# A graph network with attention on TensorE: one layer's row through DRAM, one normalisation folded into the next, and a new timetable for the attention

## The chip, the cores and the metric

The kernel runs on one core of a Trainium2 chip. The metric is the time of one launch in microseconds on the device. A core has TensorE (PE, matrix products and transposes), VectorE (DVE), ScalarE (ACT), GpSimd (POOL) and SyncE (SP, which here only issues transfers). Each works through its own list of instructions in order and waits on semaphores for the others.

## The reference

There are 64 graphs of 256 nodes with 256 features, and an adjacency matrix of zeros and ones for each. Layer 0 is a gated graph network of three steps; layer 1 is graph attention. Both are added to their input and normalised.

```python
A = (adj != 0)
h = x
for i in range(3):
    m    = h @ weight[i]
    aggr = einsum('bst,bsd->btd', A, m)
    h    = gru(aggr, h)          # r, z sigmoid; n = tanh(i_n + r * h_n); (1 - z) * n + z * h
x = layernorm(x + h)             # eps 1e-5

Wh   = x @ W
e    = leaky_relu((Wh @ a1)[:, :, None] + (Wh @ a2)[:, None, :], 0.2)
attn = softmax(where(adj > 0, e, -9e15), axis=2)
x    = layernorm(x + attn @ Wh)
```

## The kernel before

**Tiling.** Two graphs make a pair, so there are 32 pairs (`NP`) of 512 nodes. The state of a pair is kept transposed in `hT` (features on partitions, 512 nodes along the row). The product with `weight[i]` is folded into the gate weights ahead of time (`fold`, into `wc`), so that a step is an aggregation of `h` and then gate products of 512 columns. Each fp32 operand is cut into a high, a low and a cross part (`upper`, `lower`, `cross`), and a product is a sum over these.

**A block** is one step i of one pair p. `front(p, i)` prepares it: transposes to node order (`turn`), the high part (`split`), the low part (`rest`, `lo`, by POOL for i = 0), the aggregation (`aggregate`, line 340), and the parts of the aggregate and of `hT`. `gates(p, i)` then runs, for each half e of the features, the products r (12 matmuls), n (6), z (12) and t (6), all on line 369. ScalarE copies each out of PSUM (lines 374, 376) and applies sigmoid or tanh (line 387); VectorE adds the cross part (line 378); POOL and VectorE blend (lines 395 to 408).

**The order** is written out by hand. There is a clock in ticks; `at(t, step)` puts a step on a heap, and `tick()`, called after every six gate matmuls, issues all that is due. So the order on each engine is the order in which steps fall due. A block has 12 ticks. The blocks run as (turn, 0), (turn - 1, 1), (turn - 2, 2), which is 36 ticks for a pair; three pairs are under way at a time. While one block's products run, the front of the next is issued between them, by the offsets in the tuples `CLOSE` and `LOOSE`.

**Attention** of a pair starts when its last block's products are issued, and is spread over the 72 ticks that follow:

- `again` reloads the transposed input `vT` from DRAM, where `stash` had put it, and adds `hT` to it.
- `halves`, `back` and `join` turn the sum into node order `v`: both 16-bit halves are set apart, a DMA transpose on SP turns them, and they are joined again.
- `layer_norm` is called on `v`: statistics, a power on POOL (line 423), a shift, and `apply` (line 430).
- `project` (line 493) multiplies `vT` by W and by two further columns, which give s1 and s2; `spread` (lines 502, 504) scales the result by the norm's factor and copies s2, broadcast over 128 columns, into `sc`.
- `rows` (line 512) transposes these copies on TensorE, so that s2 lies along the row in every partition.
- `scores` (line 516), a mask, the row maximum (line 527) and the exponentials (line 530) follow, the last at ticks 47 and 48.
- `weights_T` (line 540) transposes the exponentials at ticks 53 and 54, `combine` (line 548) multiplies them by Wh, and a second `layer_norm` and the store follow.

PSUM has eight banks, used in rotation. Tiles of the attention lie in a pool with one buffer each (`late`; two for `v`). The last two pairs take theirs from buffers that the gates no longer need (`room`). All loads of x and adj, the stash, the reload, the DMA transposes and the store are issued by SP, in order. The weights come on ScalarE's queue and the biases on POOL's.

Of the kernel before, what the change touches and what calls it, by code (L numbers as in the profile page):

```python
# [26 lines left out]
def kernel(  # L27
# [164 lines left out]
    load_x(0)  # L192
    load_adj(0)
    make_identity(nc, ident)
    nc.gpsimd.memset(half, -0.5)
    nc.gpsimd.memset(neg, NEG_INF)
# [11 lines left out]
    def rows_T(src, use):  # L208
        for c in range(C):
            for o0, o1, t in src:  # L210
                pt = bank("pw")
                for o in range(o1 - o0):
                    nc.tensor.transpose(pt[:, o * P:(o + 1) * P], t[:, o, c * P:(c + 1) * P], ident)
                use(c, o0 * P, o1 * P, pt[:, :(o1 - o0) * P])

    def square_T(src, name):
        pt = bank("pw")
        for e in range(C):
            for d in range(C):
                nc.tensor.transpose(pt[:, (e * C + d) * P:(e * C + d + 1) * P],  # L220
                                    src[:, d, e * P:(e + 1) * P], ident)
        dst = work.tile([P, K, P], F32, tag="hi1", name=name, bufs=1)
        nc.scalar.copy(flat(dst), pt)
        return dst.rearrange("p k n -> p (k n)").rearrange("p (e d) -> p e d", e=C)

    def fold(i, wT, d):
        for o0, o1 in ((0, 512), (512, O)):
# [50 lines left out]
    def begin(p):  # L278

        s = pairs[p] = Pair()  # L280
        s.x, s.adj = loaded.pop(p), loaded_adj.pop(p)
        s.A = work.tile([P, G, C, N], F32R, tag="A", name=f"A_{p}", bufs=3)
        nc.vector.tensor_scalar(s.A, s.adj, 0.0, None, op0=ALU.not_equal)
        s.hT = work.tile([P, C, GN], F32, tag="hT", name=f"hT_{p}", bufs=4)
# [6 lines left out]
    def front(p, i, t, pace):  # L291
# [4 lines left out]
        def turn(d):  # L296
            s = pairs[p]
            if i == 0:
                src[d] = nodes(s.x, d)
# [4 lines left out]
        def split(d):  # L304
            hi[d] = work.tile([P, K, P], F32R, tag=f"hi{d}", name=f"hi{d}_{nm}", bufs=1)
            nc.scalar.copy(hi[d], src[d])

        def rest(d):
            lo[d] = work.tile([P, K, P], F32R, tag=f"lo{d}", name=f"lo{d}_{nm}", bufs=1)
            lower(nc.gpsimd if i == 0 else nc.vector, lo[d], src[d], hi[d])  # L310
# [5 lines left out]
        if i == 0:  # L316
            at(t + pace[0][1] + 2, stash)
# [92 lines left out]
    def layer_norm(v, name, t, then=None):  # L410
# [3 lines left out]
        rs = work.tile([P, K], F32, tag="rs_" + name[0], name=f"rs_{name}")  # L414
        nm = work.tile([P, K], F32, tag="nmr_" + name[0], name=f"nmr_{name}")

        def stats(k):
            nc.vector.bn_stats(st[:, k, :], v[:, k // C, k % C, :])
            nc.vector.bn_aggr(mv[:, k, :], st[:, k, :])

        def power():
            nc.gpsimd.tensor_scalar(rs, mv[:, :, 1], EPS, None, op0=ALU.add)
            nc.gpsimd.tensor_tensor(rs, rs, half, ALU.pow)  # L423

        def shift():
            nc.vector.scalar_tensor_tensor(nm, mv[:, :, 0], -1.0, rs, op0=ALU.mult, op1=ALU.mult)

        def apply(k):
            vk = v[:, k // C, k % C, :]
            nc.scalar.activation(vk, vk, AF.Identity, scale=rs[:, k:k + 1], bias=nm[:, k:k + 1])  # L430
# [9 lines left out]
        return rs  # L440

    def attention(p, t):

        s = pairs[p]
        pts = {}

# [3 lines left out]
        at(t + 5, again)  # L450
        at(t + 14, lambda: nc.vector.tensor_add(flat(s.vT), flat(s.vT), flat(s.hT)))

        def halves(d):

# [8 lines left out]
        def back(d):  # L463

            if d == 0:
                s.sc = room("sc", [P, K, N], p)
                s.turned = s.sc.rearrange("p k n -> p (k n)").bitcast(U16).rearrange(
                    "p (h k d) -> p h k d", h=2, k=K)
            nc.sync.dma_start_transpose(
                s.turned.rearrange("p h k d -> p (h k) d")[:, :, d * P:(d + 1) * P],  # L470
                s.apart[:, d].rearrange("p h n -> p (h n)"))

        def join(g):
            if g == 0:
                s.v = room("v", [P, G, C, D], p)
            dst = s.v[:, g].rearrange("p c d -> p (c d)").bitcast(U16).rearrange("p (n h) -> p n h", h=2)
            src = s.turned[:, :, g * C:(g + 1) * C, :].rearrange("p h c d -> p h (c d)")
            nc.scalar.copy(dst[:, :, 0], src[:, 0])
            nc.vector.tensor_copy(dst[:, :, 1], src[:, 1])
        for d in range(C):  # L480
            at(t + 22 + d, lambda d=d: halves(d))
            at(t + 23 + d, lambda d=d: back(d))
        for g in range(G):
            at(t + 29 + g, lambda g=g: join(g))
        at(t + 30, lambda: setattr(s, "rs", layer_norm(s.v, f"a_{p}", (t + 31, t + 33, t + 34, t + 49))))

        def project(k):
            if k == 0:
                s.s1 = work.tile([P, K], F32, tag="s1", name=f"s1_{p}")
                s.s2 = s.sc[:, :, :P]  # L490
# [14 lines left out]
        for k in range(K):  # L505
            at(t + 35 + k, lambda k=k: project(k))
            at(t + 36 + k, lambda k=k: spread(k))

        def rows():
            pts[0] = bank("s2")  # L510
            for k in range(K):
                nc.tensor.transpose(pts[0][:, k * P:(k + 1) * P], s.s2[:, k, :], ident)

        def scores():
            for k in range(K):
                nc.scalar.activation(s.sc[:, k, :], pts[0][:, (k // C) * N:(k // C + 1) * N], AF.Prelu,
                                     bias=s.s1[:, k:k + 1], alpha=ALPHA)
        at(t + 40, rows)
        at(t + 41, scores)

        s.nm = work.tile([P, K], F32, tag="nm", name=f"nm_{p}")
        s.sm = work.tile([P, K], F32, tag="sm", name=f"sm_{p}")
# [3 lines left out]
        at(t + 42, masked)  # L526
        at(t + 43, lambda: nc.vector.tensor_reduce(s.nm, s.sc, AX.X, ALU.max, negate=True))
# [28 lines left out]
        for g in range(G):  # L556
            at(t + 53 + g, lambda g=g: weights_T(g))
            at(t + 54 + g, lambda g=g: nc.vector.tensor_copy(flat(s.sc[:, g * C:(g + 1) * C, :]), pts[g]))
            at(t + 57 + g, lambda g=g: combine(g))
            at(t + 58 + g, lambda g=g: add(g))  # L560
# [4 lines left out]
        at(t + 60, lambda: layer_norm(s.v, f"b_{p}", (t + 61, t + 64, t + 66, t + 70), store))  # L565
# [3 lines left out]
    LOOSE = (2, 3, 4, 6, 7, 8), (5, 8, 10)  # L569
# [5 lines left out]


    rows_T(wh_n, lambda c, o0, o1, pt: cut_weight([t[:, c, o0:o1] for t in whh], pt, f"h{c}_{o0}"))
    begin(0)
    masking(0)
    load_adj(1)  # L580
    rows_T(wi_n, lambda c, o0, o1, pt: evacuate(wih(c, o0, o1), pt))
    nc.vector.tensor_add(b_sum, bi, bh)
    wT = square_T(w_n[0], "wT_0")
    front(0, 0, clock[0], LOOSE)
    for d in range(C):
        fold(0, wT, d)
        tick(3)
# [13 lines left out]
    for n, (p, i) in enumerate(blocks):  # L601
        if n + 1 < len(blocks):
# [43 lines left out]
```

## Time and profile before

| What | Value |
|---|---|
| time, median of 3 runs | 2247.24 us (2246.81 to 2248.58) |
| profiled execution, own time | 2248.91 us |
| its span in the profile | 2247.1 us |
| first gate product starts | 29.5 us |
| last gate product ends | 2181.1 us |
| TensorE busy | 2189.0 us (97%) |
| VectorE, ScalarE, POOL busy | 1728.2, 1556.4, 1535.2 us |

The profile shows one execution. Its own time is 1.8 us longer than its span; the difference lies around the span. "Busy" of TensorE includes time in which pipelined matmuls overlap, so costs of matmuls are read from the start of one to the start of the next. In lists of waits the columns are the total in us, how often, and the longest; in a timeline they are start and duration in us, engine, line, operation, output and input, and in brackets the idle time before with what ended it.

### The profile page before, as it was taken

To read this page: it belongs to the slowest core of one execution; us is meant where nothing else is said; L and a number is where in the kernel's file an instruction comes from. 1 tells how busy PE (TensorE), PEld (TensorE's weight loads), DVE (VectorE), ACT (ScalarE), POOL (GpSimd) and SP (SyncE) were. 2 spreads that over 40 slices of the span, in tenths; PEclk is the share of its full clock that TensorE was granted. 3 is DMA by queue.
4 is the path that set the end of the run, shared out by engine and by line. 5 is a ranking of instruction groups with operands and counts; after the bars stand their busy time and mean duration, and the time that the engine had idled before them with its cause. 6 is when DMAs were issued, how large, how long until landed. Compare 5 with 4: busy or idle time off the path is not lost.

```text
span 2247.1 us, 31126 instructions
## 1 busy us (share of the span) xinstructions
PE 2189.0 (97%) x10724; PEld 1813.6 (81%) x10724; DVE 1728.2 (77%) x2920; ACT 1556.4 (69%) x2899; POOL 1535.2 (68%) x1084
## 2 busy tenths in 40 slices
PE   7999999999999999999999999999999999999985
PEld 5788888888888888888888888888888888888864
DVE  4667778878778878778878778878778878778875
ACT  4566777677777677777677777677777677777665
POOL 5777667767667767667767667767667767667751
PEclk9999999999999999999999999999999999999997
DMA  3011111111111211112111111111111111111111
GB/s 113 29 38 38 34 42 57 57 48 38 42 43 57 57 47 38 41 45 57 57 48 38 41 45 57 57 48 38 40 46 57 57 48 38 39 47 38 29 38 47
DMA packets 130237, 105.30 MB, mean 47 GB/s; under 512 B 70368, under 2 KB 121824, under 8 KB 130080
## 3 DMA queue, kind: packets, MB, share of 16 engines
q1 hardware_dynamic: 128288, 101.47, 15.4%
q8 instruction: 86, 1.41, 0.3%
q10 hardware_dynamic: 1616, 1.57, 0.2%
q14 instruction: 71, 0.58, 0.1%
q0 software_dynamic: 176, 0.27, 0.1%
HBM read 52.96 MB, written 33.55 MB: 39 GB/s over the span
## 4 chain that ended last, share of the span: by engine, by line
PE 85%; POOL 10%; ACT 1%; DVE 1%; DMA 1%; issue 1%; POOLq 0%; SPq 0%; ACTq 0%; DVEq 0%
PE pga L369 42%; PE pgb L369 21%; PE pa L340 7%; PE po L548 5%; PE pwh L493 5%; POOL t L396 3%; PE pt L275 3%; POOL lo L132 2%; POOL t L395 2%; PE pt L540 1%; POOL n L405 1%; POOL n L401 1%; PE pt L269 1%; POOL rs_b L423 1%; DMA adj<-in_adj_dram 1%
## 5 line engine op out<-in xcount | busy, mean ns | idle before, releaser
L395 POOL TENSOR_TENSOR t<-hT,n 128x512 f32<-128x512 f32 x192 | 288.4, 1502 | 540.1 <-ACT n L387 540.0
L369 PE MATMUL pga<-hH,whhH_whh 128*128 128x512 f32 x1152 | 388.8, 418 | 0.0
L369 PE MATMUL pgb<-hD,whhD_whh 128*128 128x512 f32 x1152 | 362.0, 395 | 0.8 <-DVE hD L135 0.8
L369 PE MATMUL pga<-hL,whhL_whh 128*128 128x512 f32 x1152 | 362.3, 395 | 0.0
L405 POOL TENSOR_TENSOR n<-n,t 128x512 f32<-128x512 f32 x192 | 283.8, 1478 | 57.8 <-DVE t L378 45.5
L396 POOL TENSOR_TENSOR t<-t,z 128x512 f32<-128x512 f32 x192 | 280.6, 1461 | 15.1
L374 ACT ACTIVATE r<-pga 128x512 f32<-128x512 f32 x192 | 114.5, 596 | 235.6 <-PE pga L369 193.0
L369 PEld LDWEIGHTS pgb<-hD,whhD_whh 128*128 128x128 f32 x1152 | 216.3, 188 | 53.3 <-DVE hD L135 1.3
L369 PEld LDWEIGHTS pga<-hL,whhL_whh 128*128 128x128 f32 x1152 | 216.3, 188 | 51.6 <-POOL hL L132 0.2
L401 POOL TENSOR_TENSOR n<-n,r 128x512 f32<-128x512 f32 x192 | 252.8, 1317 | 0.8 <-DVE n L378 0.7
L132 POOL TENSOR_TENSOR hL<-hT,hH 128x1024 fp32r<-128x1024 f32 x96 | 243.8, 2540 | 8.9 <-ACT hH L129 8.9
L376 ACT ACTIVATE n<-pga,bh 128x512 f32<-128x512 f32 x192 | 131.6, 685 | 154.3 <-PE pga L369 154.0
L378 DVE SCALAR_TENSOR_TENSOR r<-pgb,r 128x512 f32<-128x512 f32 x192 | 131.7, 686 | 135.1 <-ACT r L374 75.2
L369 PEld LDWEIGHTS pga<-hH,whhH_whh 128*128 128x128 f32 x1152 | 196.0, 189 | 24.1
L340 PE MATMUL pa<-A,lo 128*128 128x256 f32 x768 | 195.9, 287 | 12.5 <-POOL lo L132 12.4
L340 PE MATMUL pa<-A,hi 128*128 128x256 f32 x768 | 196.5, 287 | 0.0
L378 DVE SCALAR_TENSOR_TENSOR n<-pgb,n 128x512 f32<-128x512 f32 x192 | 131.5, 685 | 67.5 <-ACT n L376 64.5
L387 ACT ACTIVATE z<-z,b_sum 128x512 f32<-128x512 f32 x192 | 141.6, 738 | 43.1 <-DVE z L378 42.7
L340 PEld LDWEIGHTS pa<-A,lo 128*128 128x128 f32 x768 | 146.9, 191 | 27.2 <-POOL lo L132 21.6
L378 DVE SCALAR_TENSOR_TENSOR t<-pgb,t 128x512 f32<-128x512 f32 x192 | 131.7, 686 | 38.5 <-ACT t L374 36.4
L135 DVE SCALAR_TENSOR_TENSOR hD<-hH,hT 128x1024 fp32r<-128x1024 f32 x96 | 156.5, 1630 | 0.0
L340 PEld LDWEIGHTS pa<-A,hi 128*128 128x128 f32 x768 | 146.8, 191 | 7.2
(136 smaller groups left out, 5495.6 us busy)
## 6 DMA issues: line engine op xcount, KB each, us to landing
x<-in_x_dram SPq DMA_DIRECT2D x32, 512.0 KB, 3.9
adj<-in_adj_dram SPq DMA_DIRECT2D x32, 512.0 KB, 3.9
xT<-hT SPq DMA_DIRECT2D x32, 512.0 KB, 2.6
vT<-xT SPq DMA_DIRECT2D x32, 512.0 KB, 3.3
out_dram<-v SPq DMA_DIRECT2D x32, 512.0 KB, 2.9
sc<-wh SPq DMA_TRANSPOSE x64, 3.1
w_n<-in_L_gnn_weight_dram ACTq DMA_DIRECT2D x3, 256.0 KB, 10.3
rows_aH<-in_L_gnn_w_ih_dram ACTq DMA_DIRECT2D x1, 512.0 KB, 6.1
```

The source lines that it names most:

```text
L132: eng.tensor_sub(dst, src, hi.bitcast(F32))
L135: nc.vector.scalar_tensor_tensor(dst, hi.bitcast(F32), 1.0 + U, src, op0=ALU.mult, op1=ALU.subtract)
L340: nc.tensor.matmul(pt[:, g * N:(g + 1) * N], h[:, g * C + c, :], s.A[:, g, c, :], start=(n == 0), stop=(n == len(todo) - 1))
L369: nc.tensor.matmul(pt, w[:, d, o * P:(o + 1) * P], m[:, d, :], start=n in (0, ends + 1), stop=n in (ends, len(todo) - 1))
L374: nc.scalar.activation(dst, a, AF.Copy, scale=1.0 + U)
L376: nc.scalar.activation(dst, a, AF.Identity, scale=1.0 + U, bias=bias)
L378: nc.vector.scalar_tensor_tensor(dst, b, -1.0 / U, dst, op0=ALU.mult, op1=ALU.add)
L387: nc.scalar.activation(dst, dst, func, bias=bias)
L395: nc.gpsimd.tensor_sub(t, h, n)
L396: nc.gpsimd.tensor_mul(t, t, z)
L401: after(2, lambda r=r, n=n: nc.gpsimd.tensor_mul(n, n, r))
L405: after(1, lambda n=n, t=t: nc.gpsimd.tensor_add(n, n, t))
```

## The change

1. **s2's row.** For all but the last three pairs, s1 and s2 are kept as small columns (`s12`). The s2 columns (512 elements of 4 bytes) are written to DRAM by SP, and read back broadcast to 128 partitions into `sc` (`rows`, `rows_back`). The transposes on TensorE and the broadcast copies are left out there.
2. **First norm.** `shift` and `apply` are not run on `v`. The attention's divisor is multiplied by the norm's factor instead, and the second norm's eps by its square. The second norm removes the offset.
3. **Timetable.** The ticks of the attention are given by a tuple: `EVEN` over 84 ticks for the first 29 pairs, `BRISK` for pair 29, `FAST` for pairs 30 and 31. In `EVEN` the exponentials stand at ticks 57 and 58 and `weights_T` at 60 and 61.
4. **Last three pairs.** They turn `v` back by transposes on TensorE and make s2's row as before.
5. **Fronts.** The front of a first step splits one tick or two earlier (`FIRST`), `h_cross` comes three ticks earlier, `ones` is apart from `begin`, and mask and adj load come later.
6. **Head.** x is loaded first; the front of pair 0 is interleaved with the weights' transposes; its low parts are by VectorE; an activation at the start loads the table; `fold` runs by parts; `square_T` writes to a buffer of tag "z".

```diff
+    load_x(0)
     wh_n = load_rows(w_hh, ("hH", "hL"), nc.sync)
+    load_adj(0)
     wi_n = load_rows(w_ih, ("aH", "aL"), nc.scalar)
...
-    load_x(0)
-    load_adj(0)
     make_identity(nc, ident)
     nc.gpsimd.memset(half, -0.5)
+    warm = const.tile([P, K], F32, name="warm")
+    nc.scalar.activation(warm, half, AF.Sigmoid)
...
         def rest(d):
-            lower(nc.gpsimd if i == 0 else nc.vector, lo[d], src[d], hi[d])
+            lower(nc.gpsimd if i == 0 and p else nc.vector, lo[d], src[d], hi[d])
...
         def power():
-            nc.gpsimd.tensor_scalar(rs, mv[:, :, 1], EPS, None, op0=ALU.add)
+            if eps is None:
+                nc.gpsimd.tensor_scalar(rs, mv[:, :, 1], EPS, None, op0=ALU.add)
+                nc.gpsimd.tensor_scalar(nm, rs, EPS, None, op0=ALU.mult)
+            else:
+                nc.gpsimd.tensor_add(rs, mv[:, :, 1], eps)
             nc.gpsimd.tensor_tensor(rs, rs, half, ALU.pow)
...
-        at(t[2], shift)
-        for k in range(K):
-            at(t[3] + k // 2, lambda k=k: apply(k))
-        if then:
+        if eps is not None:
+            at(t[2], shift)
+            for k in range(K):
+                at(t[3] + k // 2, lambda k=k: apply(k))
             at(t[3] + 2, then)
...
+        def back_by_pe(d):
+            pts[d] = from_T(s.vT, d)
...
         def rows():
-            pts[0] = bank("s2")
+            s.row = far.tile([K, P], F32, tag="row", name=f"row_{p}", bufs=2)
+            nc.sync.dma_start(s.row.rearrange("k n -> n k"), s.s12[:, 1, :], allow_slow_non_contiguous=True)
+
+        def rows_back():
+            pts["row"] = flat(s.sc[:, C:K, :])
+            nc.sync.dma_start(pts["row"], s.row.rearrange("k n -> (k n)").partition_broadcast(P))
+
+        def rows_by_pe():
+            s.sc = room("sc", [P, K, N], p)
+            pts["row"] = bank("s2")
             for k in range(K):
-                nc.tensor.transpose(pts[0][:, k * P:(k + 1) * P], s.s2[:, k, :], ident)
...
-            at(t + 47 + k // 2, lambda k=k: exps(k))
-        at(t + 52, lambda: nc.vector.reciprocal(s.sm, s.sm))
+            at(T["exp"] + k // 2, lambda k=k: exps(k))
+
+        def divide():
+            nc.vector.tensor_mul(s.sm, s.sm, s.rs)
+            nc.vector.reciprocal(s.sm, s.sm)
+        at(T["turn"], divide)
...
-            at(t + 53 + g, lambda g=g: weights_T(g))
-            at(t + 57 + g, lambda g=g: combine(g))
+            at(T["turn"] + g, lambda g=g: weights_T(g))
+            at(T["combine"] + g, lambda g=g: combine(g))
...
+    # again add halves join stats power project rows scores mask max exp turn combine stats2 power2 shift2 apply2
+    EVEN = 12, 21, 31, 37, 38, 40, 42, 47, 53, 55, 56, 57, 60, 64, 68, 72, 74, 81
+    BRISK = 9, 14, 15, 17, 19, 21, 30, 35, 36, 37, 38, 40, 43, 46, 49, 52, 54, 57
+    FAST = 2, 5, 6, 7, 9, 10, 14, 18, 19, 20, 20, 22, 25, 27, 30, 31, 33, 33
 
     CLOSE = (5, 5, 5, 7, 8, 8), (6, 6, 7)
-    LOOSE = (2, 3, 4, 6, 7, 8), (5, 8, 10)
+    LOOSE = (2, 3, 4, 6, 7, 8), (5, 8, 7)
+    FIRST = (2, 1, 2, 6, 7, 8), (5, 8, 7)
...
     begin(0)
+    front(0, 0, clock[0] + 1, ((0, 1, 2, 9, 11, 12), (7, 8, 13)))
+    tick(2)
+    rows_inp(wi_n[0])
+    tick()
+    rows_hid(wh_n[0])
...
-    front(0, 0, clock[0], LOOSE)
-    for d in range(C):
-        fold(0, wT, d)
-        tick(3)
+    for parts in PARTS:
+        for d in range(C):
+            fold(0, wT, d, (parts,))
+            tick(2)
...
-            front(np_, ni, clock[0], CLOSE if n and np_ == blocks[n - 1][0] else LOOSE)
+                after(4, lambda p=np_: ones(p))
+            front(np_, ni, clock[0], CLOSE if n and np_ == blocks[n - 1][0] else LOOSE if ni else FIRST)
             if ni == 0:
                 after(7, lambda p=np_: load_x(p + 1))
-                after(19, lambda p=np_: masking(p))
-                after(20, lambda p=np_: load_adj(p + 1))
+                hold = 33 if L < np_ else 16
+                after(hold, lambda p=np_: masking(p))
+                after(hold + 1, lambda p=np_: load_adj(p + 1))
...
-            attention(p, clock[0])
+            attention(p, clock[0], EVEN if p < NP - 3 else BRISK if p < NP - 2 else FAST)
```

In the lists of offsets in `FIRST`, `LOOSE` and `CLOSE` the first tuple gives turn, split, rest, aggregate, the aggregate's upper part and its rest; the second gives the upper, lower and cross parts of `hT`.

More of the change, by code (lines that the diff above doesn't have):

```diff
@@ L208, in rows_T @@
     def rows_T(src, use):
+        o0, o1, t = src
         for c in range(C):
[L210 to L214, printed above, removed]
+            pt = bank("pw")
+            for o in range(o1 - o0):
+                nc.tensor.transpose(pt[:, o * P:(o + 1) * P], t[:, o, c * P:(c + 1) * P], ident)
+            use(c, o0 * P, o1 * P, pt[:, :(o1 - o0) * P])
     def square_T(src, name):
@@ L221, in square_T, with fold @@
                                     src[:, d, e * P:(e + 1) * P], ident)
[L222 to L227, printed above, removed]
+        dst = work.tile([P, GN], F32, tag="z", name=name)
+        nc.scalar.copy(dst, pt)
+        return dst.rearrange("p (e d) -> p e d", e=C)
+    PARTS = (0, 512), (512, O)
+    def fold(i, wT, d, parts=PARTS):
+        for o0, o1 in parts:
             pt = bank("pw")
@@ L281, in begin, with ones @@
         s.x, s.adj = loaded.pop(p), loaded_adj.pop(p)
+        s.hT = work.tile([P, C, GN], F32, tag="hT", name=f"hT_{p}", bufs=4)
+    def ones(p):
+        s = pairs[p]
         s.A = work.tile([P, G, C, N], F32R, tag="A", name=f"A_{p}", bufs=3)
         nc.vector.tensor_scalar(s.A, s.adj, 0.0, None, op0=ALU.not_equal)
-        s.hT = work.tile([P, C, GN], F32, tag="hT", name=f"hT_{p}", bufs=4)
     def masking(p):
@@ L298, in turn @@
             if i == 0:
-                src[d] = nodes(s.x, d)
                 to_T(s.x, s.hT, d)
@@ L304, in split @@
         def split(d):
+            if i == 0:
+                src[d] = nodes(pairs[p].x, d)
             hi[d] = work.tile([P, K, P], F32R, tag=f"hi{d}", name=f"hi{d}_{nm}", bufs=1)
@@ L316, in front @@
         if i == 0:
-            at(t + pace[0][1] + 2, stash)
+            at(t + pace[0][0] + 3, stash)
         def h_upper():
@@ L408, in gates, with layer_norm @@
             after(lags[2], lambda n=n, t=t, h=h: nc.vector.tensor_add(h, t, n))
-    def layer_norm(v, name, t, then=None):
+    def layer_norm(v, name, t, eps=None, then=None):
         st = work.tile([P, K, nc.vector.BN_STATS_DIM], F32, tag="st_" + name[0], name=f"st_{name}")
         mv = work.tile([P, K, nc.vector.BN_AGGR_DIM], F32, tag="mv_" + name[0], name=f"mv_{name}")
-        rs = work.tile([P, K], F32, tag="rs_" + name[0], name=f"rs_{name}")
-        nm = work.tile([P, K], F32, tag="nmr_" + name[0], name=f"nmr_{name}")
+        rs = work.tile([P, K], F32, tag="rs_" + name[0], name=f"rs_{name}", bufs=3)
+        nm = work.tile([P, K], F32, tag="nmr_" + name[0], name=f"nmr_{name}", bufs=3)
         def stats(k):
@@ L434, in layer_norm, with attention, copy @@
         at(t[1], power)
-        at(t[2], shift)
-        for k in range(K):
-            at(t[3] + k // 2, lambda k=k: apply(k))
-        if then:
+        if eps is not None:
+            at(t[2], shift)
+            for k in range(K):
+                at(t[3] + k // 2, lambda k=k: apply(k))
             at(t[3] + 2, then)
-        return rs
-    def attention(p, t):
+        return rs, nm
+    def attention(p, t, pace):
         s = pairs[p]
         pts = {}
+        even = pace is EVEN
+        T = {k: t + dt for k, dt in zip(
+            "again add halves join stats power project rows scores mask max exp turn combine "
+            "stats2 power2 shift2 apply2".split(), pace)}
+        def copy(j, dst, src):
+            if even or j % 2:
+                nc.vector.tensor_copy(dst, src)
+            else:
+                nc.scalar.copy(dst, src)
         def again():
@@ L449, in again @@
             nc.sync.dma_start(s.vT, s.far)
-        at(t + 5, again)
-        at(t + 14, lambda: nc.vector.tensor_add(flat(s.vT), flat(s.vT), flat(s.hT)))
+        at(T["again"], again)
+        at(T["add"], lambda: nc.vector.tensor_add(flat(s.vT), flat(s.vT), flat(s.hT)))
         def halves(d):
@@ L466, in back @@
                 s.sc = room("sc", [P, K, N], p)
-                s.turned = s.sc.rearrange("p k n -> p (k n)").bitcast(U16).rearrange(
-                    "p (h k d) -> p h k d", h=2, k=K)
+                s.turned = flat(s.sc).bitcast(U16).rearrange("p (h k d) -> p h k d", h=2, k=K)
             nc.sync.dma_start_transpose(
@@ L475, in join, with norm @@
                 s.v = room("v", [P, G, C, D], p)
[L476 to L479, printed above, removed]
-        for d in range(C):
[L481 to L485, printed above, removed]
+            if even:
+                dst = s.v[:, g].rearrange("p c d -> p (c d)").bitcast(U16).rearrange("p (n h) -> p n h", h=2)
+                src = s.turned[:, :, g * C:(g + 1) * C, :].rearrange("p h c d -> p h (c d)")
+                nc.scalar.copy(dst[:, :, 0], src[:, 0])
+                nc.vector.tensor_copy(dst[:, :, 1], src[:, 1])
+            else:
+                copy(g, nodes(s.v, g), pts[g].rearrange("p (k n) -> p k n", k=K))
+        def back_by_pe(d):
+            pts[d] = from_T(s.vT, d)
+        for d in range(C):
+            if even:
+                at(T["halves"] + d, lambda d=d: halves(d))
+                at(T["halves"] + 1 + d, lambda d=d: back(d))
+            else:
+                at(T["halves"] + d, lambda d=d: back_by_pe(d))
+            at(T["join"] + d, lambda d=d: join(d))
+        def norm():
+            s.rs, s.eps = layer_norm(s.v, f"a_{p}", (T["stats"], T["power"]))
+        at(T["join"] + 1, norm)
         def project(k):
             if k == 0:
-                s.s1 = work.tile([P, K], F32, tag="s1", name=f"s1_{p}")
-                s.s2 = s.sc[:, :, :P]
+                s.s12 = work.tile([P, 2, K], F32, tag="s12", name=f"s12_{p}")
+                if not even:
+                    s.wh = room("wh", [P, G, C, D], p)
+                    s2 = io.tile([P, G, C, D], F32, tag="x", name=f"s2_{p}")
+                    s.s2 = s2[:, 0].rearrange("p c (h n) -> p (c h) n", n=P)
             pts[k] = bank("pwh")
@@ L497, in spread @@
             rs = s.rs[:, k:k + 1]
-            for dst, src in ((s.s1[:, k:k + 1], pts[k][:, D:D + 1]),
-                             (s.s2[:, k, :], pts[k][:, D + 1:D + 2].to_broadcast([P, P])),
-                             (s.wh[:, k // C, k % C, :], pts[k][:, :D])):
+            todo = [(s.s12[:, :, k], pts[k][:, D:D + 2]), (s.wh[:, k // C, k % C, :], pts[k][:, :D])]
+            if not even:
+                todo.insert(1, (s.s2[:, k, :], pts[k][:, D + 1:D + 2].to_broadcast([P, P])))
+            for dst, src in todo:
                 if k < 2:
@@ L505, in attention @@
         for k in range(K):
-            at(t + 35 + k, lambda k=k: project(k))
-            at(t + 36 + k, lambda k=k: spread(k))
+            at(T["project"] + k, lambda k=k: project(k))
+            at(T["project"] + 1 + k, lambda k=k: spread(k))
         def rows():
-            pts[0] = bank("s2")
-            for k in range(K):
[L512 to L522, printed above, removed]
+            s.row = far.tile([K, P], F32, tag="row", name=f"row_{p}", bufs=2)
[3 more added lines that the diff above has]
+            nc.sync.dma_start(pts["row"], s.row.rearrange("k n -> (k n)").partition_broadcast(P))
@@ new lines, in rows_by_pe, with scores @@
+        def rows_by_pe():
+            s.sc = room("sc", [P, K, N], p)
+            pts["row"] = bank("s2")
+            for k in range(K):
+                nc.tensor.transpose(pts["row"][:, k * P:(k + 1) * P], s.s2[:, k, :], ident)
+        if even:
+            at(T["rows"], rows)
+            at(T["rows"] + 1, rows_back)
+        else:
+            at(T["rows"], rows_by_pe)
+        def scores(g):
+            if g == 0:
+                s.nm = work.tile([P, K], F32, tag="nm", name=f"nm_{p}")
+                s.sm = work.tile([P, K], F32, tag="sm", name=f"sm_{p}")
+            for k in range(g * C, g * C + C):
+                nc.scalar.activation(s.sc[:, k, :], pts["row"][:, g * N:(g + 1) * N], AF.Prelu,
+                                     bias=s.s12[:, 0, k:k + 1], alpha=ALPHA)
@@ L524, in masked @@
+        for g in range(G):
+            at(T["scores"] + g * even, lambda g=g: scores(g))
         def masked():
             nc.vector.copy_predicated(flat(s.sc), flat(s.mask), neg.to_broadcast([P, K * N]))
-        at(t + 42, masked)
-        at(t + 43, lambda: nc.vector.tensor_reduce(s.nm, s.sc, AX.X, ALU.max, negate=True))
+        at(T["mask"], masked)
+        at(T["max"], lambda: nc.vector.tensor_reduce(s.nm, s.sc, AX.X, ALU.max, negate=True))
         def exps(k):
@@ L556, in attention @@
         for g in range(G):
-            at(t + 53 + g, lambda g=g: weights_T(g))
-            at(t + 54 + g, lambda g=g: nc.vector.tensor_copy(flat(s.sc[:, g * C:(g + 1) * C, :]), pts[g]))
-            at(t + 57 + g, lambda g=g: combine(g))
-            at(t + 58 + g, lambda g=g: add(g))
+            at(T["turn"] + g, lambda g=g: weights_T(g))
+            at(T["turn"] + 1 + g, lambda g=g: copy(g, flat(s.sc[:, g * C:(g + 1) * C, :]), pts[g]))
+            at(T["combine"] + g, lambda g=g: combine(g))
+            at(T["combine"] + 1 + g, lambda g=g: add(g))
         def store():
@@ L564, in store @@
             del pairs[p]
-        at(t + 60, lambda: layer_norm(s.v, f"b_{p}", (t + 61, t + 64, t + 66, t + 70), store))
+        at(T["combine"] + 3, lambda: layer_norm(
+            s.v, f"b_{p}", [T[k + "2"] for k in ("stats", "power", "shift", "apply")], s.eps, store))
+    EVEN = 12, 21, 31, 37, 38, 40, 42, 47, 53, 55, 56, 57, 60, 64, 68, 72, 74, 81
+    BRISK = 9, 14, 15, 17, 19, 21, 30, 35, 36, 37, 38, 40, 43, 46, 49, 52, 54, 57
+    FAST = 2, 5, 6, 7, 9, 10, 14, 18, 19, 20, 20, 22, 25, 27, 30, 31, 33, 33
     CLOSE = (5, 5, 5, 7, 8, 8), (6, 6, 7)
-    LOOSE = (2, 3, 4, 6, 7, 8), (5, 8, 10)
+    LOOSE = (2, 3, 4, 6, 7, 8), (5, 8, 7)
+    FIRST = (2, 1, 2, 6, 7, 8), (5, 8, 7)
     blocks = []
@@ L574, with rows_hid, rows_inp @@
         blocks += [(turn - i, i) for i in range(L) if 0 <= turn - i < NP]
-    rows_T(wh_n, lambda c, o0, o1, pt: cut_weight([t[:, c, o0:o1] for t in whh], pt, f"h{c}_{o0}"))
+    def rows_hid(part):
+        rows_T(part, lambda c, o0, o1, pt: cut_weight([t[:, c, o0:o1] for t in whh], pt, f"h{c}_{o0}"))
+    def rows_inp(part):
+        rows_T(part, lambda c, o0, o1, pt: evacuate(wih(c, o0, o1), pt))
     begin(0)
+    front(0, 0, clock[0] + 1, ((0, 1, 2, 9, 11, 12), (7, 8, 13)))
[3 more added lines that the diff above has]
+    rows_hid(wh_n[0])
+    tick()
+    rows_inp(wi_n[1])
+    tick()
+    rows_hid(wh_n[1])
+    wT = square_T(w_n[0], "wT_0")
+    nc.vector.tensor_add(b_sum, bi, bh)
+    tick()
+    ones(0)
     masking(0)
     load_adj(1)
-    rows_T(wi_n, lambda c, o0, o1, pt: evacuate(wih(c, o0, o1), pt))
-    nc.vector.tensor_add(b_sum, bi, bh)
-    wT = square_T(w_n[0], "wT_0")
-    front(0, 0, clock[0], LOOSE)
-    for d in range(C):
-        fold(0, wT, d)
-        tick(3)
+    tick()
+    for parts in PARTS:
+        for d in range(C):
+            fold(0, wT, d, (parts,))
+            tick(2)
     tick(10)
```

## The prediction

> **What bounds the kernel now.** First the page's busy table, its slices and the chain that ended last:
>
> ```profile
> PE 2189.0 (97%) x10724; PEld 1813.6 (81%) x10724; DVE 1728.2 (77%) x2920; ACT 1556.4 (69%) x2899; POOL 1535.2 (68%) x1084
> ...
> PEclk9999999999999999999999999999999999999997
> ...
> PE 85%; POOL 10%; ACT 1%; DVE 1%; DMA 1%; issue 1%; POOLq 0%; SPq 0%; ACTq 0%; DVEq 0%
> ```
>
> TensorE is busy 97% at full clock, so between first and last gate (29.5 to 2181.1 us) time changes only through TensorE instructions or TensorE waits. In the chain, the same product starts at 1053.26 and 1120.69: a pair costs 67.44 us. Next the waits of TensorE:
>
> ```profile
> PE pa L340 <- POOL lo L132: 12.4, 28, 4.3
> PE pt L540 <- ACT sc L530: 7.3, 3, 7.0
> PE pw L213 <- DMA rows_hH<-in_L_gnn_w_hh_dram: 6.4, 1, 6.4
> PE s L512 <- ACT sc L502: 5.6, 2, 5.3
> PE po L548 <- DVE sc L558: 4.4, 3, 2.3
> ```
>
> Only the first is in the steady part: one wait per pair, and one of 4.3 in the head. The others are the head (before 29.5) and the tail (after 2181.1). The timeline of TensorE prices a group of transposes and that wait:
>
> ```profile
> 1110.75 0.63 PE L369 MATMUL pga<-aH,wc0H_wc 128*128 128x512 f32 x2
> 1111.21 0.60 PE L512 MATMUL s<-ident,sc 128*128 128x128 f32 x4
> 1111.57 0.71 PE L369 MATMUL pga<-aL,wc0L_wc 128*128 128x512 f32 x2
> ...
> 1092.75 0.28 PE L340 MATMUL pa<-A,hi 128*128 128x256 f32 x1
> 1093.33 0.39 PE L340 MATMUL pa<-A,lo 128*128 128x256 f32 x1 [0.29 <-POOL lo L132]
> 1093.55 0.28 PE L340 MATMUL pa<-A,hi 128*128 128x256 f32 x1
> ```
>
> Read from start to start: a gate matmul is 0.234 us; four transposes take 0.36 and make the next pair of matmuls 0.08 later, 0.44 in all. Around the wait, hi to lo to hi takes 0.80 instead of 0.24: it costs 0.56, not the 0.29 shown as idle.
>
> Last, ScalarE's timeline around the exponentials:
>
> ```profile
> 1122.59 0.60 ACT L374 ACTIVATE z<-pga 128x512 f32<-128x512 f32 x1 [0.42 <-PE pga L369]
> 1123.21 1.28 ACT L530 ACT_TABLE_LOAD   x1
> 1124.50 0.51 ACT L530 ACTIVATE sc<-sc,nm 128x256 f32<-128x256 f32 x1
> ...
> 1126.97 1.08 ACT L430 ACTIVATE v<-v,nmr_a,rs_a 128x256 f32<-128x256 f32 x2
> 1128.07 1.28 ACT L387 ACT_TABLE_LOAD   x1
> ```
>
> Two table loads a pair, one into and one out of the exponentials; two exponentials take 1.1 with their accumulator reads.
>
> **The Trainium skill.** "ScalarE: Activation LUTs", section "What ACT_TABLE_LOAD costs", gives 1283 ns for the load and about 1380 for a drain. The trace agrees on the load (1.28) and not on the drain: 0.02 before it, 0.01 after it. I use 1.29. Its section "Table sets: the hidden batching unit" puts exp and sigmoid in different sets and tanh in both; two loads a pair agree. "DMA: Bandwidth & Descriptors", section "Rules for kernel authors", says that a strided last dimension becomes one descriptor per element, and that a read of what a DMA wrote must wait for it. The new row has 512 elements of 4 bytes; the nearest row here, a_w, also 512, took 7.0 us amid the traffic of the head. The section "Anatomy of one DMA" gives 2.0 fixed, the floor of each of the two transfers.
>
> **The change, part by part.** All against the profiled run: span 2247.1, own time 2248.9; the median of three runs is 2247.2. I apply the differences to the median.
>
> *s2 row.* Of 29 groups of L512 transposes before the last gate, 28 go (order of the two programs: 116 matmuls there before, 4 after): -28 x 0.44 = -12.2. In their place SP issues a write and a broadcast read, and the read waits on SP for the write. Behind it stand vT's reload and the adj load; both are wanted more than nine ticks (some 15 us) later. The copies of s2 that ScalarE (2 x 364 ns) and VectorE (2 x 342) made go; no matmul waited for them in the steady part. The row must land in about 11 us, from the last spread to the scores. Between 2+2 and 7.0+3.3 (the reload of vT took 3.3): it fits, at zero; not below zero, as nothing else is released.
>
> *First norm's apply left out.* -4 x 0.59 us of ScalarE a pair and one shift; one POOL product of 0.23 is added. ScalarE was 69% busy: zero on TensorE, but room.
>
> *FIRST pace.* The split and `lo` of a pair's first step come two ticks earlier for the same aggregate. POOL was late by 0.3 to 0.6; two ticks are 2.8: 27 x 0.56 = -15.1. Next late on POOL is the n,r product, which has no matmul behind it for several ticks. Between -15.1 and 0 if POOL only reorders its queue.
>
> *Exponentials in new ticks.* Before, they stood at ticks 47 and 48 and their transposes at 53 and 54; now 57 and 58, and 60 and 61. ScalarE's order there is now: n from PSUM, load, exponentials 0 and 1, load, sigmoid of r, load, exponentials 2 and 3. So four loads a pair. From the first matmul of that n product as zero: n starts at 1.12 (1139.55 to 1140.67 in the trace) and ends at 1.81; load to 3.10; two exponentials to 4.20; load to 5.50; sigmoid (0.72) to 6.23; load to 7.52; two exponentials to 8.6. TensorE does n (6 matmuls), z (12), t (6): 24 x 0.234 = 5.6, where the first transposes find exponentials 0 and 1 ready; then 0.44 and six matmuls, 1.40: at 7.45 it wants exponentials 2 and 3. It waits 1.0 to 1.1, and the restart costs 0.1 (seen at the lo wait). **A new wait of L540 on ScalarE of about 1.15 a pair**, 29 pairs: +33.4. From below: 0.8 if the next activation overlaps the one before; from above: 1.5 if n starts late. Behind the wait all gates are queued.
>
> *Last three pairs by TensorE.* More transposes before the last gate: four groups, +1.8; three project groups moved ahead of it at 0.87: +2.6. Then the tail of 66.0 us loses the three DMA transposes in a row with their copies. The last pair alone, in steps from rows of this tail (7.3 to its last hT, then 33 of add, transposes, copies, stats, power, spread, scores, mask, max, load and exponentials, combine, norm, store), is 40.5. Laid out with the two pairs before it on the same engines I get 53: -13, between -6 and -20.
>
> *Head.* x is first in the queue; `lo` of pair 0 is on VectorE, no longer behind POOL's weight scalings (4.34 wait); the table is loaded before data come. The wait for hD that set 32.8 ends at about 26: -6.5, between -3 and -9.
>
> *At nothing:* later masking, adj load and `ones`, hidden as before by the adj buffer's period; h_cross three ticks earlier, on VectorE (77%).
>
> Sum: -12.2 - 15.1 + 1.8 + 2.6 + 33.4 = +10.5 between the gates; -6.5 - 13 outside: -9.0. **2238 us.**
>
> **Rivals.**
> 1. *The exponentials are ready in time.* Then the new wait is zero and the rest stays: -22.9 - 6.5 - 13 = -42.4, 2204.8. For it: ScalarE has 31% idle and lost the applies. Against it: the chain above holds only instructions that wait for each other on one engine.
> 2. *The row is late* (ends slower). Write and read in series take over 11 us; the scores then hold up ScalarE, whose gates stand behind them, and through PSUM TensorE. At the head's 7.0 to 8.2 for such transfers (bi) plus 4.5 for a slow read (the tail's vT) that is up to 12.7: 1.7 a pair x 29 = +49 on 2238, 2287. It decides from 11.3 on: 9 us of gain over 29 pairs is 0.3. For it: 512 single elements. Against it: those times were measured amid the loads of the head.
> 3. *The wait is the longer one:* at 1.45 a pair it eats everything, 2247; above that, slower.
> 4. *The order doesn't do what it says:* POOL stays late with `lo` and the wait remains: 2238 + 15 = 2253.
>
> **How the numbers follow.** The likeliest case (wait of 0.8 to 1.3 a pair, head and tail within their bounds) has 0.58 and reaches from 2226 to 2248. Rival 1 has 0.16, rival 2 0.12, rivals 3 and 4 together 0.14. A measurement of this kernel tells about 0.2% from no change: 2242.7 to 2251.7. Of the likeliest case 0.47 is faster and 0.11 within; rival 1 is all faster; of rivals 3 and 4, 0.04 is within and 0.10 slower; rival 2 is slower. That makes 0.63, 0.15 and 0.22. The range runs from rival 1, 2203, to 2258, past rival 4; most of rival 2 and a little at the bottom are left out.
>
> **What would show it.** Right: a wait of L540's line (weights_T) on the exponentials, 29 times about 1.0; 118 table loads in place of 61; no pa wait on lo in the steady part; no transposes of s2 before pair 29; the first gate near 23 to 25 and hD before 27; a tail of 53; a period of 67.44 - 0.56 - 0.44 + 1.15 = 67.6. Wrong: a period near 66.4 (rival 1), or one above 67.8, with ScalarE's scores waiting for a DMA (rival 2), or with lo waits still there (rival 4).

## The result: slower by 8.3%

The changed kernel takes 2436.0 us (median of 4 runs, 2427.5 to 2436.8) against 2247.5 before: a ratio of 1.083, interval 1.0805 to 1.0854. The forecast was 2238. The page of the profile after, its busy line, clock and chain:

```profile
PE 2227.0 (91%) x10632; PEld 1829.2 (75%) x10632; DVE 1829.6 (75%) x2852; ACT 1560.5 (64%) x2765; POOL 1520.8 (62%) x1114
...
PEclk9999999999999999999999999999999999999998
...
PE 60%; DVE 17%; ACT 10%; POOL 7%; issue 4%; DMA 2%; POOLq 0%; DVEq 0%; ACTq 0%; SPq 0%
```

TensorE fell from 97% to 91%, and no other engine took its place: all of them wait for each other, as the chain shows, which now runs 17% through VectorE and 10% through ScalarE. TensorE's granted clock also fell: on average over the span it is 0.973 of full speed, against 0.990 before. The span times the missing share is 66 us against 22, so the clock holds at most some 43 of the 189 us, an estimate (in part of the slow time TensorE waits anyway). The waits of TensorE say for what (us in total, times, longest):

```profile
PE pt L596 <- ACT sc L581: 128.0, 82, 6.4
PE pa L347 <- DVE lo L132: 21.1, 28, 0.8
PE pgb L376 <- DVE r L385: 18.7, 28, 1.0
```

Line 596 is `weights_T`: the forecast had this wait at 29 x 1.0, and it is four times that. The other two are new. The wait of the aggregate on POOL is gone from the list. The period of a pair, from the first product with `wc0` of one to that of the next, is 74.4 us on average against 67.4.

The waits of ScalarE say why the exponentials are late, and the list of transfers (queue, count, KB each, median us to landing) has the reason:

```profile
ACT sc L570 <- DMA sc<-row: 108.8, 28, 4.5
ACT sc L581 <- DVE nm L578: 53.4, 29, 1.9
```

```profile
out_dram<-v SPq DMA_DIRECT2D x32, 512.0 KB, 10.9
sc<-row SPq DMA_DIRECT2D x29, 256.0 KB, 4.3
...
row<-s SPq DMA_DIRECT2D x29, 2.0 KB, 10.6
```

Two kilobytes take 10.6 us to DRAM, and the store of 512 KB behind them, 2.9 us before, now takes 10.9. One period on SP's queue shows the same:

```profile
1278.83 0.38 SPq L548 DMA_DIRECT2D row<-s  x1
1280.44 0.38 SPq L619 DMA_DIRECT2D out_dram<-v  x1
1289.75 0.33 SPq L552 DMA_DIRECT2D sc<-row  x1
```

SP cannot issue the read before the write has landed, 10.9 us later. ScalarE's timeline of that period, from the scores to the exponentials:

```profile
1293.42 0.91 ACT L570 ACTIVATE sc<-sc,s 128x256 f32<-128x256 f32 x2 [3.38 <-DMA sc<-row]
...
1299.37 1.28 ACT L581 ACT_TABLE_LOAD   x1
1302.53 0.51 ACT L581 ACTIVATE sc<-sc,nm 128x256 f32<-128x256 f32 x1 [1.88 <-DVE nm L578]
```

After the 3.38 us for the row, the first exponential waits 1.88 more for the row maximum. VectorE's timeline tells what stood before that:

```profile
1296.73 1.40 DVE L576 COPY_PREDICATED_SCALAR sc<-mask,neg 128x1024 f32 x1 [0.25 <-ACT sc L570]
1298.02 3.35 DVE L135 SCALAR_TENSOR_TENSOR hD<-hH,hT 128x1024 fp32r<-128x1024 f32 x1
1301.29 1.21 DVE L578 TENSOR_REDUCE nm<-sc 128x4 f32<-128x1024 f32 x1
```

Between mask and maximum stands `h_cross` (hD), moved from tick 10 to tick 7 in `LOOSE`: 3.35 us. TensorE at the end of it:

```profile
1303.90 0.63 PE L596 MATMUL pt<-ident,sc 128*128 128x128 f32 x4 [2.13 <-ACT sc L581]
...
1307.62 1.40 PE L596 MATMUL pt<-ident,sc 128*128 128x128 f32 x4 [1.17 <-ACT sc L581]
1308.67 1.20 PE L376 MATMUL pga<-aL,wc2L_wc 128*128 128x512 f32 x2
1309.67 1.05 PE L376 MATMUL pgb<-hD,whhD_whh 128*128 128x512 f32 x2
1310.52 1.05 PE L376 MATMUL pgb<-aD,wc2D_wc 128*128 128x512 f32 x2
```

Behind the second wait two gate matmuls take 0.85 us from start to start, not 0.46: TensorE runs at half its clock. The granted clock of the stretches shows how long: 1.00 from 1300 to 1304, 0.66 from 1304 to 1308, 0.50 from 1308 to 1312, 0.98 from 1312 to 1316. That is some 7 us at half clock, from about 1305.3 on: after the first wait (2.13 us) and before the second. The Trainium skill, "TensorE: Matmul & The Clock Gate", section "What's actually happening", puts this state after at least one idle window of about 3.4 us. Here less was enough: in e2 below, too, a single wait of 2.01 us (ended at 1240.55) is followed by a clock of 0.50 (1242 to 1245).

### The profile page after: what moved, and what is told of

The parts are those of the page before. It is cut to its first block, busy times and chain, and to the rows that moved or that the text cites. A ratio compares the mean times of both kernels' runs of the same rounds, so it can differ in the third digit from the quotient of the medians.

```text
span 2434.1 us, 30749 instructions
## 1 busy us (share of the span) xinstructions
PE 2227.0 (91%) x10632; PEld 1829.2 (75%) x10632; DVE 1829.6 (75%) x2852; ACT 1560.5 (64%) x2765; POOL 1520.8 (62%) x1114
## 4 chain that ended last, share of the span: by engine, by line
PE 60%; DVE 17%; ACT 10%; POOL 7%; issue 4%; DMA 2%; POOLq 0%; DVEq 0%; ACTq 0%; SPq 0%
PE pga L376 28%; PE pgb L376 14%; PE pa L347 5%; PE po L604 4%; PE pwh L528 3%; DVE wh L484 3%; ACT sc L581 3%; DVE hD L135 2%; POOL t L403 2%; ACT L581 2%; DVE st_a L426 2%; ACT r L394 2%; DVE nm L578 2%; DVE r L385 1%; ACT L394 1%
## 5 line engine op out<-in xcount | busy, mean ns | idle before, releaser
L402 POOL TENSOR_TENSOR t<-hT,n 128x512 f32<-128x512 f32 x192 | 261.6, 1363 | 557.5 <-ACT n L394 557.4
L376 PE MATMUL pga<-hH,whhH_whh 128*128 128x512 f32 x1152 | 398.0, 427 | 0.0
L412 POOL TENSOR_TENSOR n<-n,t 128x512 f32<-128x512 f32 x192 | 257.1, 1339 | 160.3 <-DVE t L385 107.5
L408 POOL TENSOR_TENSOR n<-n,r 128x512 f32<-128x512 f32 x192 | 276.6, 1441 | 3.0 <-ACT r L394 3.0
L403 POOL TENSOR_TENSOR t<-t,z 128x512 f32<-128x512 f32 x192 | 262.4, 1367 | 15.1
L132 POOL TENSOR_TENSOR hL<-hT,hH 128x1024 fp32r<-128x1024 f32 x96 | 259.0, 2697 | 15.4 <-ACT hH L129 15.3
L135 DVE SCALAR_TENSOR_TENSOR hD<-hH,hT 128x1024 fp32r<-128x1024 f32 x96 | 245.7, 2559 | 0.0
L394 ACT ACTIVATE r<-r,b_sum 128x512 f32<-128x512 f32 x192 | 139.6, 727 | 149.0 <-DVE r L385 148.6
L347 PE MATMUL pa<-A,lo 128*128 128x256 f32 x768 | 194.7, 286 | 21.2 <-DVE lo L132 21.1
L381 ACT ACTIVATE t<-pga 128x512 f32<-128x512 f32 x192 | 113.6, 592 | 125.1 <-PE pga L376 76.1
L385 DVE SCALAR_TENSOR_TENSOR z<-pgb,z 128x512 f32<-128x512 f32 x192 | 131.7, 686 | 82.2 <-ACT z L381 70.3
## 6 DMA issues: line engine op xcount, KB each, us to landing
out_dram<-v SPq DMA_DIRECT2D x32, 512.0 KB, 10.9
```

What stands on the lines that cost most here:

```text
L132: eng.tensor_sub(dst, src, hi.bitcast(F32))
L135: nc.vector.scalar_tensor_tensor(dst, hi.bitcast(F32), 1.0 + U, src, op0=ALU.mult, op1=ALU.subtract)
L347: nc.tensor.matmul(pt[:, g * N:(g + 1) * N], h[:, g * C + c, :], s.A[:, g, c, :], start=(n == 0), stop=(n == len(todo) - 1))
L376: nc.tensor.matmul(pt, w[:, d, o * P:(o + 1) * P], m[:, d, :], start=n in (0, ends + 1), stop=n in (ends, len(todo) - 1))
L381: nc.scalar.activation(dst, a, AF.Copy, scale=1.0 + U)
L385: nc.vector.scalar_tensor_tensor(dst, b, -1.0 / U, dst, op0=ALU.mult, op1=ALU.add)
```

## The experiments

Two causes were on the table: the row that lands late (R), and `h_cross` on VectorE (D); a third was the four table loads (L), which the forecast had counted.

### The row, h_cross, and both

**e1**, s2's row by TensorE again:

```diff
...
-            at(T["rows"], rows)
-            at(T["rows"] + 1, rows_back)
+            at(T["scores"] - 1, rows_by_pe)
```

> Only the way of s2's row is undone for the first 29 pairs: broadcast copies and four TensorE transposes one tick ahead of the scores, no write, no read back. Theory R (the row lands late: ScalarE stands 3.9 us a pair before the scores, the exponentials and the transposes of them follow): the DMA wait goes, 29 groups of transposes come back (+12.7), the wait of weights_T falls from 4.4 us a pair to the 1.15 forecast, the TensorE clock is whole again; 2250 us, a period near 68.0. Rival D (the h_cross product on VectorE, now between mask and maximum, makes the exponentials late): it stays, some 1.9 us a pair is saved, 2380. Rival L (four table loads a pair): it stays, not under 2390.

**e2**, h_cross back:

```diff
-    LOOSE = (2, 3, 4, 6, 7, 8), (5, 8, 7)
-    FIRST = (2, 1, 2, 6, 7, 8), (5, 8, 7)
+    LOOSE = (2, 3, 4, 6, 7, 8), (5, 8, 10)
+    FIRST = (2, 1, 2, 6, 7, 8), (5, 8, 10)
```

> Only h_cross goes back to 10 ticks in LOOSE and FIRST; the row stays in DRAM. Theory R: scores are as late as in the changed kernel, but the maximum follows the mask at once, so ScalarE's wait of 1.9 us before the first exponential goes: 1.9 us a pair and with it part of the slow clock, 2350 to 2385. Rival D (hD is the main cause): the wait of weights_T falls to about 1.2 a pair, under 2300. Rival L: no change over 10 us. VectorE's backlog before the gates of the next pair's first block (wait on r) should shrink too, if hD is part of it.

**e3**, both edits.

> Both together: row by TensorE and h_cross at 10. Theory R alone: as without the row, 2250, since hD between mask and maximum has room once scores are on time. Rival D in part: some 30 us below the kernel that only leaves out the row. Rival L: a wait of weights_T near 1.15 us a pair stays in both.

| | h_cross at 7 | h_cross at 10 |
|---|---|---|
| row through DRAM | 2436.0 | 2317.1 |
| row by TensorE | 2314.8 | 2252.3 |

Theory R alone falls: e1 was to give 2250 and gives 2314.8. Each cause alone costs 62 to 65 us, both together 184, 57 more than the sum. Late scores are made later still by hD, and the clock has a part in it: the span times the missing clock is 66 us in the changed kernel, 16 in e1 (clock 0.993), 42 in e2 (0.982) and 23 in e3 (0.990), so up to some 30 of the 57 are slow clock, an estimate. Where h_cross acts alone is told by e1's list of TensorE's waits:

```profile
PE pt L598 <- ACT sc L583: 37.0, 60, 6.4
PE pgb L376 <- DVE r L385: 29.0, 28, 1.2
PE pa L347 <- DVE lo L132: 21.1, 28, 0.8
```

`weights_T` waits there as in e3 (37.0 in both), so the maximum isn't the place; it is the cross-add of r and the low parts, which stand behind hD on VectorE. In e3 the wait on r is gone and that on lo is 2.9. The 37.0 hold 8 us of the tail; the rest is 1.0 a pair.

**e5**, only FIRST's h_cross at 10, to part the two places.

> Only FIRST's h_cross goes back to 10; LOOSE keeps 7, the row stays in DRAM. Theory B (two places: FIRST's hD falls in with halves and the second norm's statistics and makes VectorE late with the cross-add of r, so that TensorE waits for PSUM banks and for lo, 2.25 us a pair; LOOSE's hD stands between mask and maximum and makes the late scores later still, 1.95 a pair): the waits on r and lo go, the exponentials stay late; 2436 - 29 x 2.25 = 2371. Rival: all of h_cross's cost is LOOSE's: over 2420. Rival: all of it is FIRST's: 2317, as with both at 10.

It took 2363.0 where 2371 was expected, so FIRST's hD costs 73 us. The waits on r and lo fall from 18.7 and 21.1 to 0.5 and 3.7, but that of `weights_T` falls too, from 128.0 to 97.5: r and lo are not the whole of it. LOOSE's hD costs the other 46 (2363.0 to 2317.1), by the maximum: ScalarE's wait for it is 53.5 in e5 and 0.8 in e2.

**e12**, h_cross at 7 in the kernel before.

> The kernel before with h_cross at 7 in place of 10, nothing else. Theory: the harm of h_cross at 7 is a collision with the new timetable (halves and the second statistics at 31 and 32, mask and maximum at 55 and 56); in the old one mask and maximum stand at 42 and 43 and hD at 31, 43 and 55: within 5 us of before. Rival: it harms by itself (hD ahead of the cross-adds on VectorE): 2300 or more.

Theory and forecast fall here: 2289.3, 42 us slower, although mask and maximum are elsewhere. The list of TensorE's waits shows the same wait on lo as e1:

```profile
PE pa L340 <- DVE lo L132: 19.5, 28, 0.7
```

It stands in place of 8.1 us of waits on POOL's lo (12.4 less the head's 4.3); the rest of the 42 us was not traced. So h_cross three ticks earlier harms in both timetables, by 42 us in the old and 62 in the new.

### What makes the row's write slow

**e6**, the store of the pair before comes six ticks later (with h_cross at 10, as e7 and e9).

> h_cross at 10 everywhere, row in DRAM, and the store of the pair before comes six ticks later, so that it is not issued 1.6 us behind the row's write. Theory R1 (the store's packets make the write late: 10.9 us beside it, 8.5 for the first pair, which has no store behind it): the write takes 8.5, ScalarE's wait for the row falls from 3.7 to about 1.3 a pair and the time from 2317 to about 2275. Rival R2 (the write takes its time by itself, for its 512 elements): 2310 to 2320.

It took 2307.9, 9 us less. The write took 8.6 us, but the read and the store then ran into the reload of vT, and ScalarE's wait stayed (102.7 in total, 103.9 in e2):

```profile
out_dram<-v SPq DMA_DIRECT2D x32, 512.0 KB, 7.9
sc<-row SPq DMA_DIRECT2D x29, 256.0 KB, 6.2
row<-s SPq DMA_DIRECT2D x29, 2.0 KB, 8.6
```

The store explains 2 us of the write, not the rest.

**e7**, four writes of 128 elements, each a tick after its part is there:

```diff
...
-            nc.sync.dma_start(s.row.rearrange("k n -> n k"), s.s12[:, 1, :], allow_slow_non_contiguous=True)
+            nc.sync.dma_start(s.row[k:k + 1].rearrange("k n -> n k"), s.s12[:, 1, k:k + 1],
+                              allow_slow_non_contiguous=True)
...
```

> h_cross at 10 everywhere; the row is written by four transfers of 128 elements, each one tick after its part is there, the last when the whole was issued before. Theory R2 (time goes with the number of elements[...]): the last write waits for little and takes 4 to 6 us, the row is there before the scores: the wait on the row goes, 2317 - 29 x 2.25 = 2252, less the transposes' 12.7: 2240. Theory R1: still about 10, 2300 or more. If SP's further issues delay something, a wait on vT or x shows.

2262.0. Each of the four took 8.1 us in the median. ScalarE's wait fell to 64.8 in total, not to zero. The first of the four tells more. In one period it is issued at 909.75, and SP issues nothing else until 914.39:

```profile
909.75 0.32 SPq L549 DMA_DIRECT2D row<-s  x1
914.39 0.32 SPq L549 DMA_DIRECT2D row<-s  x1
...
row<-s SPq DMA_DIRECT2D x1, 0.5 KB, 7.9
```

So 128 pieces of 4 bytes still took 7.9 us, against 8.6 for 512 of them in e6.

**e9**, 128 pieces of 16 bytes:

```diff
-            s.row = far.tile([K, P], F32, tag="row", name=f"row_{p}", bufs=2)
-            nc.sync.dma_start(s.row.rearrange("k n -> n k"), s.s12[:, 1, :], allow_slow_non_contiguous=True)
+            s.row = far.tile([P, K], F32, tag="row", name=f"row_{p}", bufs=2)
+            nc.sync.dma_start(s.row, s.s12[:, 1, :])
...
```

> h_cross at 10, row in DRAM, written as 128 pieces of 16 bytes (the four values of a partition side by side) in place of 512 of 4 bytes. The row is read back in that order, so the columns of the scores are permuted: this part of the result is changed. Theory R3 (the write's time goes with the number of pieces in one transfer): [...]3.6 to 5 us; the wait for the row goes, the period is that of the row by TensorE less 0.44: 2240 us. Rival R4 (the time of such a write is fixed, as the four writes of 128 pieces at 7.8 us each suggest): a write of 8 to 10 us, 2300 or more.

2236.4, with the columns of the scores in the wrong order, which e10 below puts right. In its list of transfers:

```profile
out_dram<-v SPq DMA_DIRECT2D x32, 512.0 KB, 3.3
sc<-row SPq DMA_DIRECT2D x29, 256.0 KB, 4.9
row<-s SPq DMA_DIRECT2D x29, 2.0 KB, 1.7
```

The same 2 KB, 1.7 us in place of 10.7, and the store back from 10.7 to 3.3. The form of the write was the cause. Its number of pieces alone was not, though theory R3 had that: e7's first write has as many pieces as e9's, 128, and took 7.9 us. What is left is the size of a piece, 4 bytes or 16, and the row's order in DRAM, which e9 changes with it; the two were not parted.

### The four table loads, and a faster version

**e4**, all four exponentials at tick 57, the rest as changed:

```diff
-            at(T["exp"] + k // 2, lambda k=k: exps(k))
+            at(T["exp"] + (0 if even else k // 2), lambda k=k: exps(k))
```

> All four exponentials of a pair at tick 57, so two table loads a pair in place of four; row in DRAM and h_cross at 7 as in the changed kernel. Theory R: the first transposes of the exponentials wait as before (about 2.1 us idle), or 0.1 less; the second (1.2) no longer: with the clock that it slows, 2 to 3.5 us a pair, 2335 to 2380. Rival L (loads are the cause): both waits go, under 2290. Rival D: the same as theory R.

2396.6: 39 us less, under what theory R gave (56 to 101), and far from rival L. **e8** is the same edit on e3.

> Row by TensorE, h_cross at 10, and all four exponentials at tick 57: two table loads a pair. Theory L (what is left of the wait of weights_T in that kernel, 1.0 before the second group and 0.4 inside it, is the two further loads): both go, 29 x 1.4 = 41 less than 2252: 2211, a period near 66.6. Rival: ScalarE is late there for another reason (the exponentials start too late): the wait moves to the first group and the time stays above 2240.

2211.2, as expected: 41 us for 29 pairs is 1.41 a pair, the 0.97 and 0.43 by which TensorE's starts around `weights_T` exceed the usual in e3. Its list keeps of that wait only the tail's two:

```profile
PE pt L598 <- ACT sc L583: 8.0, 2, 6.4
```

**e10** puts the parts together: the 16-byte write, one tick of exponentials, h_cross at 10. The scores read the row with a stride, and those of the second graph go through a PSUM bank, since `sc` holds the row:

```diff
+                    if g == 1:
+                        dst = pts["s"][:, (k - C) * N:(k - C + 1) * N]
+                    dst = dst.rearrange("p (c n) -> p c n", c=C)
+                    row = pts["row"].rearrange("p (n k) -> p k n", k=K)[:, g * C:(g + 1) * C, :]
...
+                nc.vector.scalar_tensor_tensor(flat(s.sc[:, C:]), flat(s.mask[:, C:]), NEG_INF, pts["s"],
+                                               op0=ALU.mult, op1=ALU.add)
```

> A version of the whole: h_cross at 10, all exponentials at tick 57, the row written as 128 pieces of 16 bytes and read by the scores with a stride; the second graph's scores go to a PSUM bank, from which a multiply-add with the mask puts them into place. Theory R3: the version with the row by TensorE and one tick of exponentials (2211), less 29 groups of transposes (12.7), 2199. Rival R4: the row is late, ScalarE waits 2 to 4 us a pair: over 2240. If the further PSUM bank makes gates wait: 2205 to 2225.

2198.4, a ratio of 0.978 to before (0.9765 to 0.9794): faster than both kernels. Against e8 it is 12.8 us: the 29 groups of transposes at 0.44.

**e11**, e8 with FIRST's pace undone.

> The version with the row by TensorE, h_cross at 10 and one tick of exponentials, with FIRST's pace undone: the first step's split and low parts stand at 3 and 4 again. Theory: the wait of the aggregate on POOL's low parts comes back, 0.56 a pair: 2211 + 15 = 2226. Rival: POOL, without the first norm's work and with the other timetable, has lo ready anyway: 2211.

2244.4: 33 us, twice the expected, but not by the wait that was meant. POOL's lo is not late; the pace before makes a gate product wait for its PSUM bank:

```profile
PE pga L376 <- ACT r L381: 27.5, 28, 1.0
```

### A second error that hid the first

In the changed kernel, and in all made from it that keep the tile `warm`, gate matmuls start every 0.227 us (median; the pitch below), in the one before every 0.234. The changed kernel has one tile more among the constants, `warm`, which takes 32 bytes; it moves the moving operands of the gates (hH and so on) from 32 bytes past a multiple of 64 to a multiple of 64. The gates' weights lie ahead of it and stay in place.

**e13**, the kernel before with an unused tile there:

```diff
     nc.gpsimd.memset(neg, NEG_INF)
+    pad = const.tile([P, K], F32, name="pad")
+    nc.gpsimd.memset(pad, 0.0)
```

> The kernel before with one tile of 16 bytes more among the constants (it takes 32), written once and never read; all buffers behind it move by 32 bytes. In the kernel before the moving operands of the gate matmuls (hH, aH and so on) lie 32 bytes past a multiple of 64, in the changed kernel, whose tile for the early activation moved them, on one. Theory M (that shift makes a gate matmul start every 0.227 us and not every 0.234): 32 pairs x 216 x 0.007 = 48 us less, 2199, a period of 66.0. Rival (the pitch comes of the order of the work, not of the place): 2247.

2230.2, a ratio of 0.992 (0.9904 to 0.9934): 17.5 us less, pitch 0.227. **e14**, the same with 64 bytes:

> The same with a tile of 64 bytes, so that the buffers move but keep their place within 64 bytes. Theory M: 2247, pitch 0.234. Rival (any shift helps, or bank conflicts of another kind): 2200.

2248.0, pitch 0.234. **e15**, e10 with `warm`'s activation written to `b_sum` and the tile left out:

> The fastest version so far with the early activation written to b_sum in place of a tile of its own: the buffers go back by 32 bytes. Theory M: pitch 0.234, 2198 + 45 to 48 = 2245. Rival: 2198.

2215.6, 17 us more than e10, pitch 0.233. **e16**, the same edit in the changed kernel:

> The changed kernel with the same edit. Theory M: where TensorE waits for others the longer pitch is partly hidden; in the stretches without a wait it adds: 2436 + 20 to 48 = 2456 to 2484. Rival: 2436.

2435.3: nothing, where TensorE waits anyway. So the place within 64 bytes is the cause, for the two places tried; all buffers behind the tile move together. The sizes expected were too large: 48 us was the difference of medians taken over all gate matmuls. In e13 the starts from gate to gate are 0.7 us a pair closer in sum, and the wait on POOL's lo takes 0.2 of that back (17.2 us in total, 12.4 before).

## Why the prediction was wrong, point by point

- **The row at zero: this step failed.** Its upper end, 7.0 + 3.3, was taken from a_w, a load in the other direction, and fitted the 11 us by 0.7. It took 10.6 + 4.3, and e9 puts the excess on the form of the write. Rival 2 had the mechanism and the point of 11.3; it had 0.12, and 49 us. With h_cross at 10 the wait itself costs 78 us (2317.1 less 2252.3, and the 12.7 of the transposes saved on top). The forecast saw vT's reload and the adj load behind the row on SP, but not the store, which is issued 1.6 us behind it and takes 10.9 us for 2.9.
- **h_cross "at nothing": this step failed.** VectorE's 77% is an average, and a product of 2.3 to 3.4 us was put ahead of r's cross-add, the low parts and the maximum. 62 us alone, 119 beside the late row.
- **The new wait of weights_T: right in mechanism.** Forecast 1.15 a pair, 1.41 by e3 and e8. In the changed kernel the two causes above made its waits 4.1 (128.0 less the tail's 8.0, over 29 pairs).
- **The lo wait, -15.1: the wait on POOL went, the time did not come.** In e3 VectorE's low parts of a later step take its place; the starts within aggregates exceed the usual by 0.7 us a pair, 0.6 before. "Next late" was looked for on POOL alone. FIRST is worth 33 us in e11 by a PSUM bank.
- **The s2 transposes, -12.2: right,** 12.8 between e8 and e10.
- **Head and tail.** First gate at 23.0 (29.5), the wait for hD until 28.1, forecast about 26; by the second block 2.8 us are left of the forecast 6.5. From the last gate to the end some 55 against 66: -11, forecast -13.
- **The shift by 32 bytes, -17,** was in no step, and offsets what lo did not bring. So e9, the changed kernel without its two faults, lies at 2236.4, beside the forecast 2238, by luck: two errors of some 15 us in it cancel. The other terms don't close either. As measured (-12.8, +41, -2.8, -11, -17.5, and the forecast +4.4 for the last pairs) they lead from 2247.2 to 2248.5, so some 12 us of e9's time stay unassigned.

## What to carry to other kernels

A small transfer is priced by its form, not its bytes; before a row goes through DRAM in a window of fixed length, ask how small the pieces are that it is cut into, and what is issued behind it. When an instruction of some us is moved ahead on an in-order engine, list what it is now in front of, even where the engine has a quarter of its time free. And a sum that agrees isn't yet an explanation: two of its terms may be wrong.

## What was not expected of the hardware

- 512 pieces of 4 bytes from SBUF to DRAM took 8.6 us, 10.7 with a 512 KB store behind, and 128 of 4 bytes 7.9; 128 of 16 bytes took 1.5 to 1.7.
- The moving operand of a matmul of 512 columns in fp32r: 0.227 us from start to start at a multiple of 64 bytes, 0.234 at 32 past it, worth 17 us of 2247.
- Half clock on TensorE for some 7 us began after one wait of 2.1 us; in e2 it followed one of 2.0.
